# Taking the two joined steps fifth and sixth in the mixing stage, with their joining and parting cut into portions

## The chip, the cores and the metric

The kernel runs on one core of a Trainium2 chip. What is measured is the time of one execution on the device, in microseconds (us); the runs before the change have a median of 2587.52 us. The core has a matrix engine (PE, with its weight loads shown apart as PEld), a vector engine (DVE), a scalar engine (ACT), a general engine (POOL) and an engine that only issues transfers (SP). Each takes its own instructions in program order and waits on semaphores for the others.

## The reference

The input x is 4 images of 64 channels of 256 x 256, float32. Four layers follow each other. Layers 0, 2 and 3 are long separable convolutions with a filter that a small network makes, plus a per-channel multiple of the input. Layer 1 is a wavelet mixing layer, and the change lies there:

```
f1 = haar2d(x)                                  # Haar transform along both axes
acc = 0
for i in range(2):
    f3 = f1 * v[i]                              # per position
    f4 = einsum('bchw,oc->bohw', f3, conv_w[i]) # 64 x 64 over the channels
    acc += sign(f4) * relu(abs(f4) - tau[i])    # soft threshold
y = haar2d(acc, inverse=True) + x
```

## The kernel before

The four images are worked as two groups of two. Phase A does layer 0 and the forward transform, phase B the mixing of layer 1, phase C the inverse transform and layers 2 and 3. Phases A and C go by rounds of two channels, 32 rounds to a group; phase B goes by 64 steps of coefficient rows, all channels at once, so phase B of a group needs all rounds of phase A of that group, and phase C needs all of phase B. The coefficients go through DRAM in between (`coef`, `mixed`).

No scheduler orders the instructions. `beside(main, side, lead, tail)` writes the order out: it runs the main list of small pieces (a matmul block, an eviction, a few transform operations), and puts the pieces of the side list evenly in between. Phase B of group 0 is the side list of the second half of phase A (from here: **stage 0**, about 431 to 1050 us). Phase B of group 1 is the side list of phase C of group 0 (**stage 1**, about 1150 to 1900 us). In stage 0 404 side pieces lie among 270 main pieces (10 to a round); in stage 1 404 lie among 514 (18 to a round).

A step s has two units, u = 2s and 2s + 1, one for each of the two matrices. A unit u has three pieces, written u.0, u.1 and u.2:

- u.0: DVE `multiply(u)` (L626) takes the matmul result times v; DVE `less(u-1)` (L646) subtracts tau; POOL `add(u-2)` (L669 and L670 on the first unit of a step, L666 on the second) sums into the step's tile `gt`; SP stores a finished step (L675).
- u.1: PE `mix(u+1)` (L607), whose PSUM tile has one buffer, so that it waits for `multiply(u)`; ACT `sign(u)` (L632) into a tile of the ring `m` (3 buffers); DVE `threshold(u-1)` (L651); loads of v.
- u.2: ACT `magnitude(u)` (L641); on first units ACT `exchange(s)` (L657), a swap of partition halves into a tile of the ring `other` (2 buffers).

The ring `m` is freed by `add`: normally `sign(u)` takes the tile that `add(u-3)` let go. The ring `gt` has 3 buffers and is freed by the store.

Steps 0 and 1 hold coefficients for which the row transform is not finished. They are **joined** ahead of the mixing (16 DVE operations on 64 x 256, lines 579 to 586) and **parted** after it (8 POOL operations on 64 x 512, lines 592 to 599). The join is one side piece ahead of `mix(0)`. The part is in piece 6.0, in one go between `add(4)` and the next side piece, and borrows a tile of the ring `m`; the stores of steps 0 and 1 follow it.

In stage 1 the second unit of a step is left raw: the matmul result is copied to SBUF (L623), stored (L683), and thresholded in phase C. Only steps 0 and 1 have both units done in place (units 0 to 3); for them v of the second matrix is loaded into the ring `raw` at the start, and a tile of zeros (L681, a POOL memset) is stored in place of the raw result.

Main work around it: in stage 0 each round of phase A has a burst of 16 POOL operations (L344, L346), begun by the residual on DVE (L464), 1.9 us each for the first two, then shorter; DVE also evicts (L477). In stage 1 each round of phase C has 16 POOL operations of the inverse transform (L385) that grow from 0.2 to 2.5 us and end in the tile `ci`, which PE needs in the next round (L308, `c0ps`); DVE evicts the convolutions (L867).

Of the kernel before, what the change touches and what calls it, by code (L numbers as in the profile page):

```python
# [41 lines left out]
F32 = mybir.dt.float32  # L42
AF = mybir.ActivationFunctionType
ALU = mybir.AluOpType
# [3 lines left out]
P = 128  # L48
B, C, N = 4, 64, 256
# [16 lines left out]
GROUPS = 2  # L66
NB = B // GROUPS
# [3 lines left out]
PAD = 128  # L71
# [2 lines left out]
HALVES = 2 * ROUNDS  # L74
STEPS = C
FULL = 2

A_PIECES = 2 * BLOCKS + 2
C_PIECES = 4 * BLOCKS + 2
# [2 lines left out]
W = 2 * N  # L82
# [16 lines left out]
def conv_haar_kernel(  # L99
    ctx: ExitStack, tc: tile.TileContext, x, zT, w1, wbd, cols, wo, decay, wo_first, decay_first, bias, forward, inverse, wrow, pack, v, v_rows, out  # L100
):
    nc = tc.nc
# [186 lines left out]
    def half(r):  # L289
        return slice(r * ROW, (r + 1) * ROW)  # L290
# [113 lines left out]
    def run(ops, count):  # L404
        for _ in range(count):
            next(ops, None)
# [117 lines left out]
    def phase_b(grp):  # L524

        units = 2 * STEPS
        mixers = []

        def raw(u):
            return grp == GROUPS - 1 and u % 2 == 1 and FULL <= u // 2 < STEPS  # L530
        st = [dict() for _ in range(STEPS)]
        un = [dict() for _ in range(units)]
        pieces = []

        def step_of(ap, s, images):

            n = NB * W
            at = ap.offset + s // 2 * PAIR + s % 2 * P // CI * n
            rows = bass.AP(ap.tensor, at, [[n, P // CI], [STEPS // 2 * PAIR, CI], [1, n]])
            return rows, images.rearrange("p b w -> p (b w)")  # L540
# [9 lines left out]
        def load_v(s):  # L550
            if s >= STEPS:
                return
            d = st[s]
            d["v"], d["tau"] = [], []

            def fetch(first, count, tag):
                n = 2 * count * W
                t = bp.tile([P, count, 2, W], F32, tag=tag, name=f"{tag}_{grp}_{first}_{s}", bufs=3)
                at = v.offset + s * P * (4 * W + PAD) + first * 2 * W
                rows = bass.AP(v.tensor, at, [[4 * W + PAD, P], [1, n]])  # L560
                nc.sync.dma_start(t.rearrange("p i k w -> p (i k w)"), rows)
                d["v"] += [t[:, i, 0] for i in range(count)]
                d["tau"] += [t[:, i, 1] for i in range(count)]

            fetch(0, 2 if grp < GROUPS - 1 else 1, "v")
            if grp == GROUPS - 1 and not raw(2 * s + 1):
                fetch(1, 1, "raw")

        def four(name, at, b):

            tiles = [st[s][name] for s in range(2)]
            tiles.append(bp.tile([P, NB, W], F32, tag="m", name=f"spare_{name}_{grp}_{b}", bufs=3))
            return [t[at, b, bass.ts(h, N)] for t in tiles for h in range(2)]

        def join(image):

            a, b, c, d, t, u = four("f", half(image), image)
            op = nc.vector.tensor_tensor
            op(t, a, b, ALU.add)
            op(b, a, b, ALU.subtract)  # L580
            op(u, c, d, ALU.add)
            op(d, c, d, ALU.subtract)
            nc.vector.tensor_scalar(c, b, math.sqrt(2.0), None, ALU.mult)
            nc.vector.tensor_scalar(d, d, math.sqrt(2.0), None, ALU.mult)
            op(a, t, u, ALU.add)
            op(b, t, u, ALU.subtract)

        def part():

            a, b, c, d, t, u = four("g", half(0), slice(0, NB))  # L590
            op = nc.gpsimd.tensor_tensor
            op(t, a, b, ALU.add)
            op(b, a, b, ALU.subtract)
            nc.gpsimd.tensor_scalar(u, c, math.sqrt(2.0), None, ALU.mult)
            op(a, t, u, ALU.add)
            nc.gpsimd.tensor_scalar(d, d, math.sqrt(2.0), None, ALU.mult)
            op(c, b, d, ALU.add)
            op(d, b, d, ALU.subtract)
            op(b, t, u, ALU.subtract)

        def mix(u):
            s, i = divmod(u, 2)
            un[u]["f4"] = bps.tile([P, NB, W], F32, tag="f4", name=f"f4_{grp}_{u}", bufs=1)
            for b in range(NB):
                for r in range(2):
                    q = r ^ b
                    nc.tensor.matmul(  # L607
                        un[u]["f4"][half(q), b, :],
                        mixers[0][half(r), bass.ts(i, C)],
                        st[s]["f"][half(r), b],  # L610
                        start=True,
                        stop=True,
                        tile_position=(r * ROW, q * ROW),
                    )
# [28 lines left out]
        def less(u):  # L643
            if raw(u):
                return
            nc.vector.tensor_tensor(un[u]["a"], un[u]["a"], both(u, "tau"), ALU.subtract)  # L646
# [12 lines left out]
        def add(u):  # L659
            s, i = divmod(u, 2)  # L660
            if raw(u):
                un[u].clear()
                return
            m = un[u]["m"]
            if i:
                nc.gpsimd.tensor_tensor(st[s]["g"], st[s]["g"], m, ALU.add)  # L666
            else:
                g = st[s]["g"] = bp.tile([P, NB, W], F32, tag="gt", name=f"gt_{grp}_{s}", bufs=3)
                nc.gpsimd.tensor_tensor(g[:, 0], m[:, 0], st[s]["f"][:, 0], ALU.add)  # L669
                nc.gpsimd.tensor_tensor(g[:, 1], m[:, 1], st[s]["other"], ALU.add)  # L670
            un[u].clear()

        def store(s):
            to, g = step_of(mixed[grp], s, st[s]["g"])
            nc.sync.dma_start(to, g)  # L675
            st[s].clear()

        def store_raw(s):
            if s < FULL:
                t = st[s]["raw"] = bp.tile([P, NB, W], F32, tag="raw", name=f"none_{grp}_{s}", bufs=3)  # L680
                nc.gpsimd.memset(t, 0.0)  # L681
            to, g = step_of(unshrunk, s, st[s]["raw"])
            nc.sync.dma_start(to, g)  # L683

        def piece(u, j):

            s, i = divmod(u, 2)
            if j == 0:
                if u < units:
                    multiply(u)  # L690
                if 0 < u <= units:
                    less(u - 1)
                if 1 < u <= units + 1:
                    add(u - 2)
                if i == 0 and s == 3:
                    part()
                    store(0)
                    store(1)
                if i == 0 and s > 3 and not raw(2 * s - 3):
                    store(s - 2)  # L700
                if i and raw(2 * s - 1):
                    store(s - 1)
            elif j == 1:
                if u + 1 < units:
                    mix(u + 1)
                if u < units:
                    sign(u)
                if i and s < STEPS and grp == GROUPS - 1:
                    store_raw(s)
                if 0 < u <= units:  # L710
                    threshold(u - 1)
                if i == 0 and s > 0:

                    load_v(s + 2)
                    if grp < GROUPS - 1:
# [254 lines left out]
    bp = pool("b", 2, during)  # L970
# [4 lines left out]
    a, head = a[-2 * A_PIECES :], A_PIECES + BLOCKS  # L975
# [4 lines left out]
    bp = pool("b2", 2, during)  # L980
# [133 lines left out]
```

## Time and profile before

| | |
|---|---|
| runs | 2587.52, 2591.82, 2584.11 us; median 2587.52 us |
| profiled execution | 2585.35 us in all, span 2583.6 us from its first to its last instruction |
| mean granted TensorE clock | 0.977 |
| busy share of the span | PE 90%, DVE 71%, ACT 51%, POOL 80% |
| DMA, mean over the span | 265 GB/s |

The page gives busy time by engine, then the span in 40 slices of 64.6 us with the busy share of each engine in tenths. Below it is the chain that ended last, by engine: PE 60%, DVE 14%, POOL 10%, DMA 6%. Other views give the busy time of each engine in a stretch, the list of waits with their totals, and the instructions of one engine in order of time. In the timeline a line has start, duration, engine, source line, operation, tiles, and in brackets how long the engine sat idle before it and what released it. In the list of waits the numbers are the total in us, how often, and the longest.

### The profile page before, as it was taken

To read this page: it belongs to the slowest core of one execution; us is meant where nothing else is said; L and a number is where in the kernel's file an instruction comes from. 1 tells how busy PE (TensorE), PEld (TensorE's weight loads), DVE (VectorE), ACT (ScalarE), POOL (GpSimd) and SP (SyncE) were. 2 spreads that over 40 slices of the span, in tenths; PEclk is the share of its full clock that TensorE was granted. 3 is DMA by queue.
4 is the path that set the end of the run, shared out by engine and by line. 5 is a ranking of instruction groups with operands and counts; after the bars stand their busy time and mean duration, and the time that the engine had idled before them with its cause. 6 is when DMAs were issued, how large, how long until landed. Compare 5 with 4: busy or idle time off the path is not lost.

```text
span 2583.6 us, 118458 instructions
## 1 busy us (share of the span) xinstructions
PE 2319.3 (90%) x53292; PEld 1848.1 (72%) x53292; DVE 1823.0 (71%) x2049; ACT 1324.7 (51%) x2187; POOL 2064.4 (80%) x2428
## 2 busy tenths in 40 slices
PE   5999999678888888757999999999989999999999
PEld 4877877444444444546777778777789998999998
DVE  2555445799999999646677777766757777777763
ACT  1221212566666666325666666666655655655552
POOL 1898887899989999767676777766779999999991
PEclk8999999899999999978999999999999999999999
DMA  7676998699999999555988999988876666666653
GB/s 210 216 244 234 298 309 283 243 342 323 337 340 316 351 321 330 182 194 194 331 301 309 317 320 323 313 306 297 288 233 211 223 213 212 221 216 208 219 166 111
DMA packets 203676, 685.23 MB, mean 265 GB/s; under 512 B 29289, under 2 KB 30826, under 8 KB 190755
## 3 DMA queue, kind: packets, MB, share of 16 engines
q1 hardware_dynamic: 203171, 677.67, 77.1%
q8 instruction: 418, 6.85, 1.1%
q14 instruction: 87, 0.71, 0.1%
HBM read 427.93 MB, written 249.63 MB: 262 GB/s over the span
## 4 chain that ended last, share of the span: by engine, by line
PE 60%; DVE 14%; POOL 10%; DMA 6%; issue 5%; ACT 3%; SPq 2%; DVEq 0%; ACTq 0%; POOLq 0%
PE c2c L296 11%; PE c2r L296 10%; PE c1r L296 9%; PE c1c L296 9%; PE a1ps L296 6%; PE a2ps L296 6%; PE f L607 4%; PE c0ps L308 4%; POOL fw L344 3%; DVE m L651 3%; POOL f L346 3%; DVE x L626 3%; DVE a L646 2%; PE a3ps L308 2%; DVE x L464 2%
## 5 line engine op out<-in xcount | busy, mean ns | idle before, releaser
L385 POOL TENSOR_TENSOR i<-i,g 128x16 f32<-128x16 f32 x744 | 431.5, 601 | 27.7 <-ACT g L362 0.6
L296 PEld LDWEIGHTS a2ps<-toep,ay 64*64 64x64 f32 x8192 | 305.5, 137 | 163.9 <-DVE f L477 86.4
L296 PE MATMUL a2ps<-toep,ay 64*64 64x128 f32 (+3 forms) x8192 | 357.7, 306 | 47.9 <-DVE f L477 42.3
L607 PE MATMUL f<-ft,mix 64*64 64x512 f32 x2048 | 297.3, 617 | 111.6 <-DVE x L626 94.3
L296 PEld LDWEIGHTS a1ps<-toep,x 64*64 64x64 f32 x8192 | 288.4, 134 | 89.7 <-issue 45.4
L296 PE MATMUL a1ps<-toep,x 64*64 64x64 f32 (+3 forms) x8192 | 337.6, 300 | 16.6 <-DMA x<-in_x 11.4
L296 PEld LDWEIGHTS c2c<-toep,ch 64*64 64x64 f32 x8192 | 300.0, 135 | 58.9 <-issue 19.1
L296 PE MATMUL c1r<-toep,z 64*64 64x192 f32 (+3 forms) x8192 | 319.0, 300 | 22.6 <-issue 11.9
L296 PEld LDWEIGHTS c1c<-toep,ch 64*64 64x64 f32 x8192 | 296.2, 134 | 57.8 <-issue 18.5
L296 PEld LDWEIGHTS c1r<-toep,z 64*64 64x64 f32 x8192 | 292.4, 135 | 59.2 <-issue 28.0
L296 PE MATMUL c2c<-toep,ch 64*64 64x256 f32 (+3 forms) x8192 | 314.7, 299 | 8.4 <-ACT ch L848 6.8
L296 PE MATMUL c1c<-toep,ch 64*64 64x128 f32 (+3 forms) x8192 | 310.3, 298 | 9.0 <-ACT ch L848 5.5
L669 POOL TENSOR_TENSOR gt<-m,ft 128x512 f32<-128x512 f32 x128 | 163.5, 1277 | 193.7 <-DVE m L651 188.8
L385 POOL TENSOR_TENSOR ci<-i,g 128x1024 f32<-128x1024 f32 x124 | 313.9, 2552 | 4.5
L444 ACT COPY ay<-a1ps 128x512 f32<-128x512 f32 x256 | 137.4, 589 | 351.2 <-PE a1ps L296 350.6
L296 PEld LDWEIGHTS c2r<-toep,cy 64*64 64x64 f32 x8192 | 287.9, 134 | 32.9 <-issue 15.2
L632 ACT ACTIVATE m<-x 128x1024 f32<-128x1024 f32 x194 | 206.1, 1062 | 205.3 <-DVE x L626 98.5
L296 PE MATMUL c2r<-toep,cy 64*64 64x192 f32 (+3 forms) x8192 | 310.1, 297 | 1.3 <-issue 1.1
L848 ACT COPY ch<-c2r 128x512 f32<-128x512 f32 x256 | 137.3, 591 | 280.2 <-PE c2r L296 279.5
L477 DVE TENSOR_TENSOR f<-a3ps,wrow_sb 128x512 f32<-128x512 f32 x256 | 161.3, 683 | 130.2 <-PE a3ps L308 130.2
L626 DVE TENSOR_TENSOR x<-f,v 128x1024 f32<-128x1024 f32 x192 | 233.5, 1216 | 22.1 <-PE f L607 20.5
L344 POOL TENSOR_TENSOR fw<-x 128x1024 f32<-128x1024 f32 x64 | 122.2, 1910 | 150.4 <-DVE x L464 137.9
(83 smaller groups left out, 3976.8 us busy)
## 6 DMA issues: line engine op xcount, KB each, us to landing
toep<-filt SPq DMA_DIRECT2D x384, 224.0 KB, 5.3
ft<-coef SPq DMA_DIRECT2D x128, 512.0 KB, 7.6
v<-in_v SPq DMA_DIRECT2D x64, 1024.0 KB, 10.1
mixed<-gt SPq DMA_DIRECT2D x128, 512.0 KB, 7.2
g<-mixed SPq DMA_DIRECT2D x256, 256.0 KB, 5.1
x<-in_x SPq DMA_DIRECT2D x128, 256.0 KB, 4.4
coef<-f SPq DMA_DIRECT2D x128, 256.0 KB, 4.0
x<-in_x SPq DMA_DIRECT2D x32, 1024.0 KB, 8.0
```

The costliest lines, as they stand in the source:

```text
L296: nc.tensor.matmul(ps[r][half(c), j % 2, k * ROW :], data[half(r), c, k, bass.ts(j, ROW)], t(r, c)[:, : N - k * ROW], start=k == 0, stop=k ...
L308: nc.tensor.matmul(ps[r][half(c)].rearrange("p h k -> p (h k)"), matrix[half(r)], pairs(r, c).rearrange("p h k -> p (h k)"), start=True, s ...
L344: nc.gpsimd.tensor_tensor(diffs, even, odd, ALU.subtract)
L346: nc.gpsimd.tensor_tensor(sums, even, odd, ALU.add)
L385: engine.tensor_tensor(to, s, d, op)
L444: later(lambda y=y, ps=ps: nc.scalar.copy(y, ps))
L477: later(lambda f=f, ps=ps, w=w: nc.vector.tensor_tensor(f, ps, w, ALU.mult))
L607: nc.tensor.matmul(un[u]["f4"][half(q), b, :], mixers[0][half(r), bass.ts(i, C)], st[s]["f"][half(r), b], start=True, stop=True, tile_posi ...
L626: nc.vector.tensor_tensor(un[u]["x"], un[u]["f4"], both(u, "v"), ALU.mult)
L632: nc.scalar.activation(un[u]["m"], un[u]["x"], AF.Sign)
L669: nc.gpsimd.tensor_tensor(g[:, 0], m[:, 0], st[s]["f"][:, 0], ALU.add)
L848: later(lambda y=y, ps=ps: nc.scalar.copy(y, ps))
```

## The change

The order of the steps becomes 2, 3, 4, 5, 0, 1, 6, ... 63. The two joined steps are then at positions 4 and 5 (`held`), units 8 to 11. Every load and store addresses a step through `order`. `join` and `part` become generators. The join runs 4 operations at a time in pieces 6.0, 6.1, 6.2 and 7.0; the part runs 2 at a time in pieces 13.1, 13.2, 14.0 and 14.1, and both stores follow in 14.2. The join's spare tile comes from the ring `other` and is allocated once, with one image's room; the part's spare still comes from the ring `m`. In stage 1 units 1, 3, 5 and 7 are now raw and units 8 to 11 are done in full; v of the second matrix for the two steps is loaded in pieces 7.2 and 9.2 rather than at the start. The side list has 403 pieces.

```diff
+LATE = 4
@@ phase_b
+        order = [*range(FULL, FULL + LATE), *range(FULL), *range(FULL + LATE, STEPS)]
+        held = range(LATE, LATE + FULL)
         def raw(u):
-            return grp == GROUPS - 1 and u % 2 == 1 and FULL <= u // 2 < STEPS
+            return grp == GROUPS - 1 and u % 2 == 1 and 0 < u < units and u // 2 not in held
...
-            n = NB * W
+            n, s = NB * W, order[s]
...
-            if grp == GROUPS - 1 and not raw(2 * s + 1):
-                fetch(1, 1, "raw")
...
+        def four(name, at, b, spare):
+            rows = [(st[s][name], b) for s in held] + [(spare, slice(0, spare.shape[1]) if b == slice(0, NB) else 0)]
+            return [t[at, b, bass.ts(h, N)] for t, b in rows for h in range(2)]
+        def join():
+            spare = bp.tile([P, 1, W], F32, tag="other", name=f"spare_f_{grp}", bufs=2)
             op = nc.vector.tensor_tensor
-            op(t, a, b, ALU.add)
+            for image in range(NB):
+                a, b, c, d, t, u = four("f", half(image), image, spare)
+                yield op(t, a, b, ALU.add)
+                yield op(b, a, b, ALU.subtract)
+                yield op(u, c, d, ALU.add)
+                yield op(d, c, d, ALU.subtract)
+                yield nc.vector.tensor_scalar(c, b, math.sqrt(2.0), None, ALU.mult)
+                yield nc.vector.tensor_scalar(d, d, math.sqrt(2.0), None, ALU.mult)
+                yield op(a, t, u, ALU.add)
+                yield op(b, t, u, ALU.subtract)
...
         def part():
+            spare = bp.tile([P, NB, W], F32, tag="m", name=f"spare_g_{grp}", bufs=3)
+            a, b, c, d, t, u = four("g", half(0), slice(0, NB), spare)
             op = nc.gpsimd.tensor_tensor
-            op(t, a, b, ALU.add)
+            yield op(t, a, b, ALU.add)
...
         def piece(u, j):
-                if i == 0 and s == 3:
-                    part()
-                    store(0)
-                    store(1)
-                if i == 0 and s > 3 and not raw(2 * s - 3):
+                if i == 0 and s > 1 and s - 2 not in held and not raw(2 * s - 3):
                     store(s - 2)
...
+                if i and s + 1 in held and grp == GROUPS - 1:
+                    fetch(s + 1, 1, 1, "raw")
+            if u == 2 * LATE - 2 and j == 0:
+                joining.append(join())
+            if u // 2 == LATE - 1:
+                run(joining[0], 4)
+            at = 3 * (u - 2 * (LATE + FULL) - 1) + j - 1
+            if at == 0:
+                joining.append(part())
+            if 0 <= at < 4:
+                run(joining[1], 2)
+            if at == 4:
+                for k in held:
+                    store(k)
...
-        pieces += [start] + [lambda: None] * 10 + [lambda: [join(b) for b in range(NB)], lambda: mix(0)]
+        joining = []
+        pieces += [start] + [lambda: None] * 10 + [lambda: mix(0)]
```

More of the change, by code (lines that the diff above doesn't have):

```diff
@@ L552, in load_v @@
                 return
[L553 to L563, printed above, removed]
@@ L565, in load_v @@
-            fetch(0, 2 if grp < GROUPS - 1 else 1, "v")
-            if grp == GROUPS - 1 and not raw(2 * s + 1):
-                fetch(1, 1, "raw")
[L569 to L577, printed above, removed]
-            op = nc.vector.tensor_tensor
[L579 to L586, printed above, removed]
+            st[s]["v"], st[s]["tau"] = [], []
@@ new lines, in load_v, with fetch @@
+            fetch(s, 0, 2 if grp < GROUPS - 1 else 1, "v")
+        def fetch(s, first, count, tag):
+            d, n = st[s], 2 * count * W
+            t = bp.tile([P, count, 2, W], F32, tag=tag, name=f"{tag}_{grp}_{first}_{s}", bufs=3)
+            at = v.offset + order[s] * P * (4 * W + PAD) + first * 2 * W
+            rows = bass.AP(v.tensor, at, [[4 * W + PAD, P], [1, n]])
+            nc.sync.dma_start(t.rearrange("p i k w -> p (i k w)"), rows)
+            d["v"] += [t[:, i, 0] for i in range(count)]
+            d["tau"] += [t[:, i, 1] for i in range(count)]
@@ L588, in part @@
         def part():
-            a, b, c, d, t, u = four("g", half(0), slice(0, NB))
+            spare = bp.tile([P, NB, W], F32, tag="m", name=f"spare_g_{grp}", bufs=3)
+            a, b, c, d, t, u = four("g", half(0), slice(0, NB), spare)
             op = nc.gpsimd.tensor_tensor
-            op(t, a, b, ALU.add)
[L593 to L596, printed above, removed]
@@ L597, in part @@
-            op(c, b, d, ALU.add)
-            op(d, b, d, ALU.subtract)
-            op(b, t, u, ALU.subtract)
+            yield op(t, a, b, ALU.add)
+            yield op(b, a, b, ALU.subtract)
+            yield nc.gpsimd.tensor_scalar(u, c, math.sqrt(2.0), None, ALU.mult)
+            yield op(a, t, u, ALU.add)
+            yield nc.gpsimd.tensor_scalar(d, d, math.sqrt(2.0), None, ALU.mult)
+            yield op(c, b, d, ALU.add)
+            yield op(d, b, d, ALU.subtract)
+            yield op(b, t, u, ALU.subtract)
@@ L678, in store_raw @@
         def store_raw(s):
-            if s < FULL:
+            if s in held:
                 t = st[s]["raw"] = bp.tile([P, NB, W], F32, tag="raw", name=f"none_{grp}_{s}", bufs=3)
```

## The prediction

> **What bounds the kernel.** I read the busy times by stretch first, to see which engine fills which stage, then the waits of both stages, then the timelines round the join and the part. Columns of the stretches: PE, PEld, DVE, ACT, POOL busy, then PE clock, DMA share, GB/s.
>
> ```profile
> 431.00:470.00 39.00, 29.48 (x496) 19.64 (x492) 33.84 (x46) 18.78 (x24) 25.36 (x34) 0.91 0.84 310
> 470.00:520.00 50.00, 32.89 (x488) 19.80 (x484) 35.64 (x37) 24.47 (x31) 45.52 (x52) 0.86 0.65 243
> 700.00:800.00 100.00, 81.68 (x1326) 49.33 (x1324) 95.64 (x100) 64.59 (x81) 91.13 (x105) 0.98 0.95 337
> 1150.00:1220.00 70.00, 54.52 (x1120) 42.62 (x1120) 51.55 (x51) 43.13 (x75) 53.84 (x49) 0.89 0.63 211
> 1300.00:1400.00 100.00, 92.44 (x2163) 73.34 (x2155) 70.40 (x67) 63.01 (x111) 71.09 (x82) 1.00 0.89 307
> ```
>
> Stage 0 is bound by DVE (95.6 of 100 us) with POOL (91) and the DMA (0.95) close behind. Stage 1 is bound by PE (92); DVE and POOL have 30% free. The first two rows and the fourth show what the beginning of each stage loses.
>
> ```profile
> ACT m L632 <- POOL gt L670: 37.0, 25, 6.5
> DVE a L646 <- ACT a L641: 32.8, 38, 6.0
> ACT m L632 <- POOL gt L599: 6.5, 1, 6.5
> ```
>
> ```profile
> PE c0ps L308 <- POOL ci L385: 10.0, 1, 10.0
> PE f L607 <- DVE ft L586: 2.1, 2, 1.8
> ```
>
> In stage 0 the two 6.5 us waits of ACT for a tile of ring m (add(4) at 476.7, the part's last operation at 487.6) make DVE idle 5.74 and 5.96 us in the timeline. In stage 1 PE waits 10.0 us for ci, which stands behind the part on POOL:
>
> ```profile
> 1200.40 1.28 POOL L670 TENSOR_TENSOR gt<-m,other 128x512 f32<-128x512 f32 x1
> ...
> 1213.11 1.26 POOL L599 TENSOR_TENSOR gt<-_slice(0, 2, None)_16315 64x512 f32<-64x512 f32 x1
> 1214.34 3.51 POOL L385 TENSOR_TENSOR i<-i,g 128x512 f32<-128x512 f32 x2
> 1217.93 4.64 POOL L385 TENSOR_TENSOR ci<-i,g 128x1024 f32<-128x1024 f32 x2
> ```
>
> So both waits are real. The question is what replaces them. The join of stage 1 shows it, DVE first, POOL below:
>
> ```profile
> 1156.11 1.35 DVE L584 TENSOR_SCALAR ft<-ft 64x256 f32<-64x256 f32 x1
> 1157.38 1.49 DVE L585 TENSOR_TENSOR ft<-spare_f 64x256 f32<-64x256 f32 x1
> 1158.79 2.58 DVE L586 TENSOR_TENSOR ft<-spare_f 64x256 f32<-64x256 f32 x1
> 1161.40 0.42 DVE L579 TENSOR_TENSOR spare_f<-ft 64x256 f32<-64x256 f32 x1
> ```
>
> ```profile
> 1156.01 2.58 POOL L385 TENSOR_TENSOR i<-i,g 128x512 f32<-128x512 f32 x2
> 1158.66 2.42 POOL L385 TENSOR_TENSOR ci<-i,g 128x1024 f32<-128x1024 f32 x1
> ```
>
> Operations that take 0.29 to 0.42 us alone last until the POOL operation beside them ends; at 1161.4, with POOL idle, they are short again. The first image took 9.3 us, the second 2.9.
>
> [...]
>
> **Stage 0, part by part.** (a) Start. PE waited for the join until 438.31 and DVE multiplied at 440.31. Now mix(0) needs ft alone (landed about 432.2: issue 424.6, 7.4 to 7.7 us), but multiply(0) needs v, and the load issued at 427.9 took 13.0 us; the one ahead of it, 1 MB less at 419 GB/s, lands about 438.2. So 2.1 us at once; while DVE is short of work (3.2 us idle up to 467) PE's lead brings some 2 more. Take -4.0 (bounds -2, -6). (b) DVE's stalls go: 5.74 + 5.96, and 1.47 for a v load that stood behind the stores on SP (SP waited 20.1 us for L599): -13.2. (c) The join's 16 operations return in 6.0 to 7.0, where DVE is the bound: +5.9 (432.38 to 438.26). (d) [...] Piece 6.0 falls, by 403 side pieces on 270, on the main piece that begins the POOL burst. Behind the residual DVE does threshold, multiply, less (3.5 us); then POOL is at the end of its second 1.9 us operation, and 1.04, two of 1.27 (add(4)), 1.04, 0.61, 0.61, 0.4 ... and add(5) with 2.4 follow. Alternating one by one, the portions wait 0.3 + 1.04 + 1.27 + 1.27, then 0.5 + 0.6 + 0.4 + 0.4, then 0.3 + 2.4 + 0.3 + 0.25, then nothing (POOL waits for threshold(6)): +9.0 (bounds 0, +16: every operation behind one of 1.0 us). (e) The part, 10.9 us on POOL (476.66 to 487.56), in 13.1 to 14.1. Its place is kinder, behind the burst instead of in it, but sign(14) now takes the tile of add(12), which stands behind four part operations. POOL's sum from the burst's start: burst 4.85 + 2.26 + 1.1 + 0.78 + 0.45 + 0.42, add(9) to add(11) 7.3, four part operations 5.3, add(12) 2.55: 25.0 us. DVE comes to less(14), 13 side pieces of 1.65 us and one multiply later, at 22.7 and can go on at 25.0 + 2.1 (sign, magnitude): 4.4 us. sign(15) waits for the last part operation (30.3), about 1 us more, the next burst 0.6. Take +6.0 (bounds +2, +11). exchange(3) waits for add(4) (ring other) at 8.7 us, when ACT has nothing due: 0. Behind the held stores on SP (14.2) stand x, v and ft loads wanted a round or two units later; the wait, about 11 us, is shorter than the 20.1 before: 0. Step 7's gt tile waits for a store of 7 us under add(13) and a burst of 7.2: 0. Sum: -4.0 - 13.2 + 5.9 + 9.0 + 6.0 = **+3.7 us**.
>
> **Stage 1.** (f) PE's waits that go: 2.1 for the join, 10.0 for ci, about 2 for multiply at 1184 to 1211 (1.17, 0.61, 0.29), since units 1, 3, 5 are raw and POOL sheds two L666 (4.7) and the part (12.7): -14.1. (g) The join in 6.0 to 7.0 lies, by 403 on 514, on main pieces 11, 12, 14, 15 of a round, where POOL does its operations of 0.74, 1.5, 1.5, 2.4, 2.4. multiply(6) comes at 1192.2 (before: mix(6) on PE from 1194.6 to 1195.7, now 3.5 earlier by the terms of (f)). From 1193.4 the first portion waits 0.5 + 1.5 + 1.5 + 2.4 and works 1.6: 1200.9. The second waits once more, 2.4, and works 1.3: 1204.6. The third has POOL idle, 1.7: 1206.3. multiply(7), a raw copy, ends at 1207.5. mix(8) waits for it; PE has done three of its four c1c blocks by 1200.6 (before 1204.6): idle 6.9 us. mix(9) waits 2.3 more, behind the fourth portion, threshold(6) and two pairs of evictions: +9.2 (bounds 0, +16). (h) Units 8 to 11 in full: 4 x (1.23 + 1.62 + 1.59) = 17.7 us of DVE plus 5 of evictions in 22 us (four units of 5.5), where PE had no wait before: +1; v of the second matrix is issued 1.8 us behind the raw copy of unit 7, lands 5.8 to 7.6 us later, wanted after 11: +1 (0 to 3). Zero tiles, 2 x 0.95 on POOL, fit. (i) The part falls on pieces 3 to 7 of a round, where inverse operations are 0.3 us; POOL has 30% free for 12 pieces, ci is due 5 pieces later: 0 (up to 4). Sum: -14.1 + 9.2 + 2.0 = **-2.9 us**.
>
> Together +0.8 on the profiled 2585.35 us: 2586.1; that execution is 2.2 below the median of the runs shown, so I say **2587 us**.
>
> **Rivals.** *Faster*: DVE gets its short operations in between at nearly no cost, or POOL is not in long operations when they come. Without (d) stage 0 gives -5.3; without (g) stage 1 gives -12: 2585.4 - 17 = 2568 to 2570. For it: at 432 to 435, beside 0.25 us POOL operations, each join operation took 0.41 us. Against: the four lines above. *Slower*: [...] +7 and +7 over the forecast, 2601: one mechanism, in 6.0 to 7.0, deciding once a join operation loses over about 0.8 us on average (9.0 / 16 = 0.56 in the forecast for stage 0). For it: 2.58 us for one of 0.42. Against: POOL idles behind add(5). *Part at full price*: POOL's 9% of slack in stage 0 takes none of it up, (e) is 11: 2592. For it: two stalls of 11.7 us from 10.9 us of work before. Against: its place behind the burst.
>
> **Numbers.** Forecast (own range 2579 to 2596) 0.42, faster rival 0.30, slower 0.18, full price 0.10. A run of this kernel can't tell 0.3%, 7.8 us, from no change. The faster rival lies beyond it, the slower one too; of the forecast and the full price 0.10 runs over upwards. So faster 0.30, same 0.42, slower 0.28. The range, 2569 to 2602, leaves out about half of the faster rival's spread and a little above.
>
> **What would show it.** Join operations of 0.4 to 2.5 us at unit 6 in both stages, DVE without a gap there; PE waiting about 7 us for L623 before the eighth mix of stage 1; no 10 us wait for ci; one DVE gap of 4 to 5 us beside the part in stage 0 and none of PE in stage 1. Wrong if join operations keep to 0.42 us (then 2570), or if the multiplication of the first unit in stage 0 comes well before 438.

## The result, and the profile after

The changed kernel takes 2618.74 us (median of 4 runs, 2612.46 to 2621.67) against 2585.82 us before on the same chip (4 runs): a ratio of 1.0132, 95% interval 1.0108 to 1.0156. That is slower by about 33 us; forecast was 2587 us, no change, with a range that ended at 2602. The profiled execution took 2619.38 us (span 2616.3 us), 34.0 more than the one before.

The stretches of the kernel after, with the columns of those of before (stretch, length, then busy PE, PEld, DVE, ACT, POOL, then PE clock, DMA share, GB/s):

```profile
431.00:470.00 39.00, 24.12 (x456) 15.07 (x456) 34.28 (x34) 20.14 (x25) 28.00 (x29) 0.95 0.92 339
470.00:520.00 50.00, 32.79 (x500) 18.69 (x504) 45.10 (x52) 23.23 (x29) 36.08 (x43) 0.84 0.62 226
700.00:800.00 100.00, 72.74 (x1270) 49.42 (x1261) 88.35 (x91) 58.89 (x74) 82.35 (x89) 0.91 0.87 308
800.00:900.00 100.00, 80.80 (x1329) 47.95 (x1333) 95.82 (x100) 65.63 (x81) 91.11 (x102) 1.00 0.93 328
1150.00:1220.00 70.00, 52.54 (x1031) 42.41 (x1035) 27.29 (x31) 34.57 (x70) 38.58 (x62) 0.85 0.67 227
1250.00:1350.00 100.00, 81.19 (x1841) 62.26 (x1837) 67.97 (x58) 57.25 (x101) 86.03 (x79) 0.93 0.76 266
1300.00:1400.00 100.00, 92.46 (x2091) 71.25 (x2091) 65.81 (x62) 59.90 (x106) 70.71 (x83) 0.95 0.92 327
```

Between 470 and 520 us DVE now works 45 us where it worked 36: the stalls that the forecast wanted gone are gone. But between 700 and 800, far behind the last joined or parted tile, DVE is down from 95.6 to 88.4 us and POOL from 91 to 82, and from 800 on both are back. A stretch in which no joined or parted tile is worked has become slower. In stage 1 the stretch 1250:1350 has POOL at 86 and PE at 81 us, where the kernel before had 70 and 95:

```profile
1250.00:1350.00 100.00, 94.56 (x2202) 78.24 (x2202) 68.29 (x68) 63.75 (x112) 69.94 (x78) 1.00 0.88 305
```

The waits of PE in the kernel after from 1150 to 1400 us say why (total, times, longest):

```profile
PE c0ps L309 <- POOL ci L386: 10.6, 1, 10.6
PE f L609 <- DVE raw L625: 9.6, 4, 6.1
```

The wait for `ci` that was to go is there again, 79 us later in the span (1301.7 us against 1222.6).

Where the difference arises shows best along one sequence of instructions that both kernels have. Start of the same residual of phase A (four to a round) or of phase C (eight to a round), after less before, worked out from the two traces:

| place | difference |
|---|---|
| residual A 132 (420 us), ahead of all that differs | -3.9 us |
| multiply of unit 0 | -5.7 |
| residual A 148 / 152 (520 / 544 us; in between lies the part) | -4.5 / +4.6 |
| residual A 188 / 252 (756 / 1114 us) | +24.1 / +24.1 |
| residual C 0, about 1135 us | +23.8 |
| residual C 16 / 32 (1228 / 1280 us in the kernel before) | +15.3 / +28.0 |
| residual C 496 (2555 us in the kernel before) | +32.8 |

The first row says that this execution was 3.9 us ahead before it came to anything that differs. The executions of the other kernels below stand between 2.7 us ahead and 1.4 behind at that point. Such a lead is carried along: in the four of them whose stage 0 is that of the kernel before, it changes by 1.0 to 1.4 us until the end of stage 0. So what stage 0 costs is counted from residual A 132 here, and what stage 1 costs from residual C 0. Stage 0 costs 28.0 us (-3.9 to +24.1): the beginning, up to residual A 152, where all the moved work lies, 8.5, and the rounds behind it 19.5. Stage 1 costs 9.0.

**What slows the quiet rounds.** From 598 to 756 us six rounds of phase A take 26.1 to 26.3 us instead of 23.5 to 23.7. Four more take 24.8 to 25.0: the two ahead of them, the one behind them, and one at 491 us. The order of the operations on DVE within a round differs (rr two residuals, t threshold, x multiply, l less, ff two evictions, read off the timelines):

```
before                  rr t x l rr t x l t x l t ff x l ff t x l
after, 549 to 598 us    rr x l t rr x l t x l t x l ff t ff x l t
after, 598 to 756 us    rr x l t rr x l t x l t ff x l t ff x l t
after, from 780 us      rr t x l rr t x l t x l t ff x l ff t x l
```

The timelines of one such round of the kernel after, DVE first, then POOL, then ACT (start, duration, operation, and in brackets the idle time before it and what ended it):

```profile
623.46 1.23 DVE L653 SCALAR_TENSOR_TENSOR m<-a,m 128x1024 f32<-128x1024 f32 x1
624.60 1.40 DVE L465 SCALAR_TENSOR_TENSOR x<-x,bias_sb,a2ps 128x512 f32<-128x512 f32 x2
625.92 1.22 DVE L628 TENSOR_TENSOR x<-f,v 128x1024 f32<-128x1024 f32 x1
627.05 1.22 DVE L648 TENSOR_TENSOR a<-a,v 128x1024 f32<-128x1024 f32 x1
628.39 1.23 DVE L653 SCALAR_TENSOR_TENSOR m<-a,m 128x1024 f32<-128x1024 f32 x1
629.53 1.40 DVE L465 SCALAR_TENSOR_TENSOR x<-x,bias_sb,a2ps 128x512 f32<-128x512 f32 x2
...
643.58 1.23 DVE L648 TENSOR_TENSOR a<-a,v 128x1024 f32<-128x1024 f32 x1 [3.06 <-ACT a L643]
```

```profile
624.83 2.36 POOL L668 TENSOR_TENSOR gt<-gt,m 128x1024 f32<-128x1024 f32 x1 [0.63 <-DVE m L653]
631.00 1.89 POOL L345 TENSOR_TENSOR fw<-x 128x1024 f32<-128x1024 f32 x1 [3.82 <-DVE x L465]
```

```profile
640.60 1.06 ACT L634 ACTIVATE m<-x 128x1024 f32<-128x1024 f32 x1 [3.74 <-POOL gt L672]
```

A round of the kernel before, the burst on POOL and the only stretch in which DVE idles:

```profile
617.41 2.37 POOL L666 TENSOR_TENSOR gt<-gt,m 128x1024 f32<-128x1024 f32 x1 [0.61 <-DVE m L651]
620.98 1.89 POOL L344 TENSOR_TENSOR fw<-x 128x1024 f32<-128x1024 f32 x1 [1.20 <-DVE x L464]
...
632.60 1.23 DVE L646 TENSOR_TENSOR a<-a,v 128x1024 f32<-128x1024 f32 x1 [0.92 <-ACT a L641]
```

In the kernel after, POOL's last sum before its burst is let go by the threshold at 623.46, and the burst itself by the second pair of residuals, at 629.53. In between DVE has a pair, a multiply, a less, a threshold and the pair itself; in the good order that stretch is a multiply, a less and the pair. One pair (1.40) and one threshold (1.23) more are 2.6 us, and POOL idles 3.82 us ahead of the burst where it idled 1.20 before. The late burst pushes the sums behind it, the sign on ACT waits 3.74 us for one of them, the less on DVE 3.06 us for the magnitude that follows, where it waited 0.92 before: so the round closes 2.6 us late, and the next begins in the same order. In the order of the second row the same wait of DVE is 1.86 to 2.00 us, and the round 1.3 us longer. This chain of waits is read off the timelines; what the experiments test is the order. Six times 2.6 and four times 1.3 come to 20.8 of the 28.0 us.

The order is that of the list. `beside` places 403 side pieces on 270 where it placed 404. The content of a piece sits one place earlier at the front of the list, two thirds of a main piece, and drifts to no offset at its end; until about 755 us that is enough to bring three thresholds of a round ahead of a pair of residuals or evictions that they stood behind.

### The profile page after: what moved, and what is told of

It is laid out like the page before. It is cut to its first block, busy times and chain, and to the rows that moved or that the text cites. A ratio compares the mean times of both kernels' runs of the same rounds, so it can differ in the third digit from the quotient of the medians.

```text
span 2616.3 us, 118463 instructions
## 1 busy us (share of the span) xinstructions
PE 2303.0 (88%) x53292; PEld 1870.1 (71%) x53292; DVE 1831.1 (70%) x2049; ACT 1324.6 (51%) x2187; POOL 2060.6 (79%) x2428
## 4 chain that ended last, share of the span: by engine, by line
PE 60%; DVE 16%; POOL 10%; DMA 5%; issue 5%; ACT 2%; SPq 1%; DVEq 0%; ACTq 0%; POOLq 0%
PE c2r L297 10%; PE c2c L297 10%; PE c1r L297 10%; PE c1c L297 9%; PE a1ps L297 6%; PE a2ps L297 5%; PE f L609 4%; PE c0ps L309 4%; DVE x L628 3%; POOL fw L345 3%; POOL f L347 3%; DVE a L648 3%; DVE m L653 3%; PE a3ps L309 2%; DVE x L465 2%
## 5 line engine op out<-in xcount | busy, mean ns | idle before, releaser
L609 PE MATMUL f<-ft,mix 64*64 64x512 f32 x2048 | 311.7, 635 | 144.4 <-DVE x L628 129.0
L297 PE MATMUL a2ps<-toep,ay 64*64 64x128 f32 (+3 forms) x8192 | 341.2, 305 | 34.0 <-DVE f L478 29.0
L297 PEld LDWEIGHTS c1c<-toep,ch 64*64 64x64 f32 x8192 | 304.2, 134 | 54.0 <-issue 23.3
L297 PEld LDWEIGHTS a1ps<-toep,x 64*64 64x64 f32 x8192 | 278.8, 134 | 85.6 <-issue 44.4
L297 PE MATMUL a1ps<-toep,x 64*64 64x64 f32 (+3 forms) x8192 | 323.0, 300 | 14.2 <-DMA x<-in_x 11.0
L297 PEld LDWEIGHTS c1r<-toep,z 64*64 64x64 f32 x8192 | 299.1, 135 | 50.4 <-issue 24.0
L297 PE MATMUL c1c<-toep,ch 64*64 64x192 f32 (+3 forms) x8192 | 314.3, 298 | 9.0 <-ACT ch L861 6.1
L297 PE MATMUL c2c<-toep,ch 64*64 64x128 f32 (+3 forms) x8192 | 314.7, 298 | 8.1 <-ACT ch L861 7.1
L297 PE MATMUL c2r<-toep,cy 64*64 64x128 f32 (+3 forms) x8192 | 311.1, 297 | 4.2 <-issue 4.2
```

What stands on the lines that cost most here:

```text
L297: nc.tensor.matmul(ps[r][half(c), j % 2, k * ROW :], data[half(r), c, k, bass.ts(j, ROW)], t(r, c)[:, : N - k * ROW], start=k == 0, stop=k ...
L609: nc.tensor.matmul(un[u]["f4"][half(q), b, :], mixers[0][half(r), bass.ts(i, C)], st[s]["f"][half(r), b], start=True, stop=True, tile_posi ...
```

## The experiments

Times are medians, ratios are to the kernel before on the same chip, with the 95% interval.

**Is it the count of pieces?** Two edits, one to each kernel. The rival was a lag that the part leaves behind.

```diff
 the changed kernel, 404 side pieces
-        pieces += [start] + [lambda: None] * 10 + [lambda: mix(0)]
+        pieces += [start] + [lambda: None] * 11 + [lambda: mix(0)]
 the kernel before, 403 side pieces
-        pieces += [start] + [lambda: None] * 10 + [lambda: [join(b) for b in range(NB)], lambda: mix(0)]
+        pieces += [start] + [lambda: None] * 9 + [lambda: [join(b) for b in range(NB)], lambda: mix(0)]
```

> The changed kernel with one more empty side piece ahead of mix(0), in both stages, so that each side list has 404 pieces again and every unit stands beside the main pieces that it stood beside before; the join and the part move with it. Theory A (places): the slow rounds of stage 0 (about 26 us each for phase A rounds 38 to 47, instead of 23.6) come from where the 403 pieces fall among the main pieces, which gives DVE and ACT another order. Then all rounds of stage 0 but those with the join and the part take 23.6 us, stage 0 is within 8 us of before, and the ratio to the kernel before is 1.002 to 1.006. Theory B (lag): POOL, 10.9 us late by the part while it is 91% busy, stays late and keeps the rounds slow. Then they are slow here too and the ratio is 1.010 to 1.014.

> The kernel before with one empty side piece fewer in both stages, and nothing else changed: join and part as before, 403 pieces. Theory A (places): the same order of DVE and ACT as in the changed kernel, slow rounds until about round 47, stage 0 +20 to +30 us, ratio 1.007 to 1.012. Theory B (lag): the part is where it was, so nothing keeps the rounds slow: ratio 0.998 to 1.002.

An empty piece more: 2597.75 us, 1.0050 (1.0032 to 1.0069). An empty piece less in the kernel before, nothing else: 2609.11 us, 1.0108 (1.0075 to 1.0141). The stretches 700 to 800 us, the changed kernel with 404 first, the kernel before with 403 second:

```profile
700.00:800.00 100.00, 81.69 (x1326) 49.32 (x1324) 95.58 (x100) 64.58 (x81) 91.22 (x105) 0.98 0.95 337
```

```profile
700.00:800.00 100.00, 71.90 (x1233) 48.05 (x1227) 87.77 (x91) 58.92 (x74) 82.31 (x93) 0.91 0.87 303
```

The first is the row of the kernel before, nearly to the digit; the second that of the kernel after. With 404 POOL's wait ahead of the burst is back to that of the kernel before:

```profile
617.37 2.37 POOL L668 TENSOR_TENSOR gt<-gt,m 128x1024 f32<-128x1024 f32 x1 [0.61 <-DVE m L653]
620.93 1.90 POOL L345 TENSOR_TENSOR fw<-x 128x1024 f32<-128x1024 f32 x1 [1.19 <-DVE x L465]
```

This is shown, then. One empty piece less costs stage 0 of the kernel before 22.8 us (1.9 ahead at residual A 132, 20.9 behind at 252), in rounds of the same orders and lengths as in the kernel after; one more brings stage 0 of the changed kernel from 28.0 down to 2.7 (2.7 ahead to level). Of these 25.3 us the ten rounds above are 20.8, and 4.5 lie in the round with the join (residual A 140 to 144: 36.6 us with 403, 32.2 with 404). In stage 1 the count isn't the cause: the kernel before with 403 is 20.7 us behind at residual C 0 and at C 496. The lag of the part as a cause falls, since in the kernel before with 403 the part is where it was and the slow rounds come all the same.

**Each group alone.** The edit makes the lag of the held steps a value of the group, 4 in one and 0 in the other; a group with lag 0 keeps the join as a piece of its own ahead of `mix(0)`, and so 404 pieces, and the part in piece 6.0.

```diff
+        lag = LATE if grp in (0,) else 0        # and (1,) in the second kernel
-        order = [*range(FULL, FULL + LATE), *range(FULL), *range(FULL + LATE, STEPS)]
-        held = range(LATE, LATE + FULL)
+        order = [*range(FULL, FULL + lag), *range(FULL), *range(FULL + lag, STEPS)]
+        held = range(lag, lag + FULL)
...
```

> The change in group 0 alone; group 1 (stage 1) has the order, the join, the part and the 404 pieces of the kernel before. Both theories: stage 0 is 24 us longer, stage 1 as before: ratio 1.008 to 1.010. If stage 1 only inherits a loss from stage 0, the whole 1.013.

> The change in group 1 alone; group 0 (stage 0) is as before. Stage 1 loses about 8 us by the trace of the changed kernel (PE waits 6 us for the raw copy behind the join and 10.6 us for ci behind the part, and saves 10 us elsewhere): ratio 1.002 to 1.005. If the loss of stage 1 came from a late start in stage 0, 0.998 to 1.001.

Group 0 alone: 2615.78 us, 1.0128 (1.0103 to 1.0153), more than the 1.008 to 1.010 expected. Its stage 0 costs 28.4 us (0.2 ahead at residual A 132, 28.1 behind at 252), like that of the kernel after; the 24 us of the expectation were too few by the early lead. Stage 1 inherits no loss, though the ratio is the one forecast for that: the trace loses nothing behind residual C 0 (+28.4 there, +25.3 at C 496). Group 1 alone: 2594.54 us, 1.0043 (1.0013 to 1.0072), as expected. The two add up to 1.0171, more than the 1.0132 of both together, which the intervals allow. In stage 1 the second kernel leads by 12.1 us at residual C 16 (3.0 of it at C 0 already) and has lost it at 32 (+0.6); it ends 5.4 us behind. PE's waits from 1150 to 1600 us in it have the loss:

```profile
PE c0ps L309 <- POOL ci L386: 10.6, 1, 10.6
PE f L615 <- DVE x L634: 7.7, 9, 2.9
...
PE f L615 <- DVE raw L631: 5.9, 4, 4.5
```

**What stage 1 pays for.** Group 1 alone again, once without the part and once without the join of its two held steps.

```diff
 without the part
-            if 0 <= at < 4:
+            if 0 <= at < 4 and not grp:
 without the join
-            if u // 2 == LATE - 1:
+            if u // 2 == LATE - 1 and not grp:
```

> The change in group 1 alone, with the part of group 1's two held steps left out: their results are stored unparted, and the 8 POOL operations (10.5 us) of stage 1 are gone. Without that cut the same kernel stood at 1.0043 of before; in its profile it led by 12.1 us at residual C 16, and behind the PE wait of 10.6 us on the inverse (c0ps on ci) it was 0.6 us behind at residual C 32. Theory C (the part's POOL time is what stage 1 pays: it keeps the inverse, and so PE, waiting): the wait on ci of about 10 us is gone, residual C 32 leads by 8 to 12 us, and most of that lasts to the end: 0.996 to 1.000 of before. Theory D (the wait on ci belongs to the second round of phase C, as in the kernel before, which has one of 10.0 us without any part near it; the part lies in its shadow): the wait stays at 8 us or more and the ratio at 1.003 to 1.005.

> The change in group 1 alone, with the join of group 1's two held steps left out: the 16 DVE operations between the pieces of stage 1 are gone, the part is done. Theory C (the part is what stage 1 pays): the PE waits on the raw copies (5.9 us with the join) go, but the wait on ci of about 10 us stays; ratio 1.001 to 1.004 of before. Rival [...]: the wait on ci falls under 4 us and the ratio to 0.996 to 1.000.

Without the part: 2582.06 us, 0.9972 (0.9954 to 0.9989). The same list of waits holds none for `ci`; residual C 16 to 32 loses 3.5 us where it lost 12.7 with the part, and the lead at C 32 is 6.8 us (2.9 of it at C 0 already), a little less than theory C gave. At C 496 2.4 are left:

```profile
PE c1r L297 <- ACT z L861: 10.9, 1, 10.9
PE f L615 <- DVE x L634: 8.3, 9, 2.5
...
PE f L615 <- DVE raw L631: 6.6, 4, 4.6
```

Without the join: 2586.64 us, 0.9992 (0.9979 to 1.0005). The waits on the raw copies fall from 5.9 to 1.0 us, the one on `ci` stays at 10.6. The ratio lies a little under what theory C gave, so the join costs somewhat more than its waits on PE; but the wait on `ci` is the part's, so D falls, and the rival, by which the join holds the inverse back, too. D's ground was not so either: in the kernel before the part ends at 1214.4 us, just ahead of the inverse that PE waits for until 1222.6, so that the wait there stood behind a part as well.

**Can stage 0 keep its lead?** With 404 pieces stage 0 leads by 9.1 us at residual A 148 and by 0.1 at 152, with the part in between: it costs 9.0 (the 7.6 us at residual A 144, of which the expectations speak, are not yet the whole lead). Two kernels with 404 pieces: the part cut into 16 operations over eight pieces with a spare tile of its own, and the part of group 0 left out.

```diff
 part over eight pieces
-            spare = bp.tile([P, NB, W], F32, tag="m", name=f"spare_g_{grp}", bufs=3)
+            spare = bp.tile([P, 1, W], F32, tag="spare", name=f"spare_g_{grp}", bufs=1)
+            for image in range(NB):             # the eight operations for each image
...
-            if 0 <= at < 4:
+            if 0 <= at < 8:
...
-            if at == 4:
+            if at == 7:
 no part in group 0
-            if 0 <= at < 4:
+            if 0 <= at < 4 and grp:
```

> The changed kernel with 404 side pieces, and its part cut into 16 operations for one image each, two to a piece over eight pieces (13.1 to 15.2) instead of two whole ones to a piece over four, with a spare tile of its own that takes no slot of ring m; the stores go out in the last of the eight pieces. With the part in four pieces this kernel stood at 1.005: stage 0 led by 7.6 us at residual A 144 and by 0.1 at 152. Theory E (the part costs by its lumps: a burst of phase A that waits behind two long operations and a slot of ring m that is held): stage 0 keeps 4 us or more of the lead, ratio 1.001 to 1.003. Theory F (POOL is 91% busy in stage 0, so 10.5 us more on it fit nowhere within a few rounds): the lead at residual A 160 is 0 to 2 us, ratio 1.004 to 1.006.

> The changed kernel with 404 side pieces and with the part of group 0's two held steps left out: they are stored unparted, and stage 0 loses 8 POOL operations (10.5 us). With the part it stood at 1.005, and the lead of 7.6 us at residual A 144 was gone at 152. If the part alone takes the lead back (theories E and F alike), the lead of about 7.5 us stands from residual A 152 to the end of stage 0, and the ratio falls by 7.5/2585 to about 1.002. If the lead is lost to a standing order of the two instruction streams that any delay falls back to, it is gone here too, and the ratio stays at 1.005.

Over eight pieces: 2595.75 us, 1.0035 (1.0023 to 1.0046); residual A 152 is 3.1 us *behind*, so theory E falls and stage 0 pays 11.8 us for the part (8.7 ahead at residual A 148), more than F's forecast of a lead of 0 to 2 us. The ratio doesn't tell it from the kernel with four pieces, since the intervals overlap. Without the part: 2586.52 us, 0.9995 (0.9978 to 1.0011), below the 1.002 expected; the lead of 6.9 us stands from residual A 148 to the end of stage 0, so no standing order takes it. The profiled execution of that kernel took 2592.6 us, 6 more than its median: differences along a trace tell where time goes, the ratios how much. Small differences that gather slowly tell nothing: the kernel with 404 pieces and this one have the same stage 1, and from residual C 32 to C 496 the first loses 4.5 us and the second 7.3; group 0 alone, whose stage 1 is that of the kernel before, gains 4.1 there.

**Is there a place where the two are free?** If POOL's 30% of slack in stage 1 (busy 71 of 100 us between 1300 and 1400) could swallow the part anywhere but beside an early round, the middle of the stage should do; and the end of stage 0 should be free of the full engines.

```diff
+        lag = (0, 30)[grp]                      # and (62, 30) in the second kernel
...
-        pieces += [start] + [lambda: None] * 10 + [lambda: mix(0)]
+        pieces += [start] + [lambda: None] * (11 if lag else 10) + [lambda: run(join(), 16)] * (not lag) + [lambda: mix(0)]
...
 second kernel, part of group 0: four operations to a piece
+            at *= 1 + (lag > LATE and not grp)
-                run(joining[1], 2)
+                run(joining[1], 4 if not grp else 2)
```

> The change in group 1 alone, with the two held steps 31st and 32nd of group 1 instead of fifth and sixth, and 404 side pieces there; group 0 as before. At fifth and sixth this stood at 1.0043: it gained 9 to 12 us at the start of stage 1 and lost them to the part beside the second round of phase C (wait on ci 10.6 us). Theory C' (the part only costs there because it meets the inverse of a round whose PE work is due; in the middle of the stage POOL is 71 to 74% busy and swallows it): the lead of about 10 us at residual C 16 stands at residual C 32 and 48, the wait on ci is under 4 us, and at most 5 us are lost near 1500 us: 0.996 to 0.999 of before. Theory G (the lead isn't worth anything by itself: the second round of phase C and the rounds behind it end when their own inputs allow): residual C 48 is within 3 us of before, ratio 0.999 to 1.003.

> As the kernel with 31st and 32nd in group 1, and in group 0 the two held steps are last (63rd and 64th), with 404 side pieces; the part of group 0 then runs four operations to a piece behind the last sums of the stage. With the part left out of group 0, stage 0 kept a lead of 6.9 us. Theory F (in stage 0 DVE is 95% and POOL 91% busy, so join and part cost what they take wherever they are, except behind the stage's last pieces): stage 0 leads by 7 us at residual A 152 and keeps 3 to 7 us of it; then 0.994 to 0.998 of before. Rival (the end of stage 0 is as dear as its start, since phase A's last rounds and phase C's first loads wait there for the stores of the held steps): the lead at residual C 0 is within 2 us of the kernel with group 0 as before, and the ratio is no lower than that kernel's.

Middle of stage 1: 2593.10 us, 1.0036 (1.0020 to 1.0052); both theories fall. The lead is 17.8 us at residual C 16, 23.0 at 96 (1466 us), still 11.4 behind the join (1475 to 1491 us) and gone behind the part (1532 to 1547 us): +3.0 at 128. The wait on `ci` has moved with the part; none of 10 us is left at the second round (PE, 1150 to 1600 us):

```profile
PE c0ps L309 <- POOL ci L386: 13.0, 2, 12.3
```

End of stage 0 as well: 2601.91 us, 1.0067 (1.0039 to 1.0095). Here stage 0 leads by 14.6 us with neither join nor part done, evenly from residual A 152 to 232; since it was 1.4 behind at A 132, 16.0 are gained. The join near the end takes 13.8 and the part 10.9 more, so that stage 0 ends 10.0 us behind. The part then stands ahead of a burst of phase A, and PE waits for it, in 1050 to 1150 us:

```profile
PE a2ps L297 <- DVE f L478: 18.0, 3, 10.2
PE a3ps L309 <- POOL fw L347: 8.3, 1, 8.3
```

Theory F falls in its exception, the quiet end. Its rival is right on the ratio, and short on the size: the start of phase C is 10.9 us later than with group 0 as before, not within 2.

**Less work in place of another place.** If the two cost what they take of DVE and POOL, then taking operations off these engines should pay. The scalings by the root of two go to ACT, which is busy about 65% of stage 0 (64.6 of 100 us between 700 and 800), in the kernel before and in the changed one with 404 pieces.

```diff
-            nc.vector.tensor_scalar(c, b, math.sqrt(2.0), None, ALU.mult)
-            nc.vector.tensor_scalar(d, d, math.sqrt(2.0), None, ALU.mult)
+            nc.scalar.mul(c, b, math.sqrt(2.0))
+            nc.scalar.mul(d, d, math.sqrt(2.0))
...
-            nc.gpsimd.tensor_scalar(u, c, math.sqrt(2.0), None, ALU.mult)
+            nc.scalar.mul(u, c, math.sqrt(2.0))
...
-            nc.gpsimd.tensor_scalar(d, d, math.sqrt(2.0), None, ALU.mult)
+            nc.scalar.mul(d, d, math.sqrt(2.0))
```

> The kernel before, with the scalings by the root of two on ACT: four of the join's 16 operations per group leave DVE (0.29 us each) and two of the part's 8 leave POOL (1.49 us each); places unchanged. Theory H (join and part cost close to what they take of DVE and POOL wherever they stand): 3 us per part and up to 1 us per join less, so about 6 to 8 us for both groups: 0.997 to 0.9985 of before. Rival (the chain of the part gets a crossing between two engines at each scaling and ACT's signs wait behind it): 1.000 to 1.003.

> The changed kernel with 404 side pieces and the scalings of join and part on ACT. With the scalings on DVE and POOL it stood at 1.005. Theory H: the part takes back 3 us less of stage 0's lead (residual A 152 at about -3 us) and the wait on ci in stage 1 shrinks from 11.3 us to about 8: ratio 1.001 to 1.003. Rival (crossings and ACT's queue): 1.004 to 1.007.

The kernel before with it: 2578.99 us, 0.9984 (0.9970 to 0.9998), the lowest ratio of any kernel here that does the whole computation, and small. The changed one with 404: 2587.96 us, 1.0014 (0.9997 to 1.0032), from 1.0050. In its trace residual A 152 leads by 3.7 us (about 3 expected): the part costs 6.0 us from residual A 148 where it cost 9.0. The wait on `ci` is 7.9 us (about 8 expected). One part scaling takes 0.63 us on ACT where it took 1.49 on POOL. Both ratios lie where theory H put them, and the rival falls, in the kernel before by little.

## Why the prediction was wrong

**The step that failed** is the sum for stage 0, in what it left out. It priced the pieces that hold join and part, (a) to (e), and put every other round at nothing without a reason; it used 403 on 270 only to find where piece 6.0 falls. The same division moves all other pieces too. The missing term is 20.8 us in ten rounds without join or part, of 32.9 in all; with nothing changed but the count it is 22.8. The order on DVE in a round, and how long POOL idles ahead of each burst, could have been worked out from the kernel's list and the page before, since the two numbers 404 and 403 and the durations 1.40 and 1.23 were all there. In stage 1 it was step (i).

**Priced steps of stage 0.** Forecast +3.7. Measured, up to residual A 152: 8.5 in the kernel after, 2.6 with 404 pieces. That the sum is right to about 1 us where the order of the pieces is kept is luck: there (a) to (d) come out 4.1 us better than forecast and (e) 3.0 worse.

- (a) Start: -4.0 forecast, 2.1 of it at once. At once it was 1.8, the -5.7 less the 3.9 of before (1.7 to 2.2 in the six other kernels with the moved join). The v tile landed at 434.6, that is 438.5 without the early lead, where 438.2 was forecast. So the sign of being wrong that the forecast named, a multiplication well before 438, came true by the early lead alone.
- (b) The stalls of 5.74 and 5.96 us went, as said.
- (c) and (d) The join and its waits for POOL: 14.9 us forecast (5.9 + 9.0). The 16 operations took 13.7 us in all, and stretched as said; DVE of the kernel after:

```profile
462.98 1.92 DVE L580 TENSOR_TENSOR spare_f<-ft 64x256 f32<-64x256 f32 x1
...
471.17 0.41 DVE L586 TENSOR_TENSOR ft<-spare_f 64x256 f32<-64x256 f32 x1
...
473.03 2.56 DVE L582 TENSOR_TENSOR spare_f<-ft 64x256 f32<-64x256 f32 x1
475.63 0.42 DVE L583 TENSOR_TENSOR ft<-ft 64x256 f32<-64x256 f32 x1
```

  The same operation is 0.42 us where POOL is in short operations (0.47 us from 475.27, then 0.33) and 2.56 beside a sum of 2.54 on POOL (L668, from 472.77). The estimate of the forecast, that a join operation lasts about until the POOL operation beside it ends, was within 1.2 us in all. Other operations on DVE kept their length in stage 0: the threshold (L653), whose input `a` is in PSUM there, took 1.21 to 1.23 us each of 128 times, and in stage 1, where it reads `x` in SBUF, up to 3.37 us; no run here tells whether the place of the input is the cause. The faster rival, by which the join operations keep to about 0.42 us, is out.
- (a) to (d) together: -2.3 forecast. Measured at residual A 148: -0.5, with 1.3 of the slower order in it; -6.4 with 404 pieces.
- (e) Part: +6.0 forecast, 9.0 measured from residual A 148 to 152, in the kernel after and with 404 pieces alike. The idle stretch of DVE beside the part is 5.84 us (4.4 forecast); the one in the next burst is 3.22, where 0.6 was added.

**Stage 1.** Forecast -2.9, measured about +9.

- (f), (g): -4.9 forecast together; measured -8.5 from residual C 0 to 16. The wait of PE for the raw copy ahead of mix(8) was 6.1 us (6.9 forecast), all four 9.6 (9.2 forecast). That (g) came so near is partly luck. The join's 16 operations were stretched to 9.7 us from the 6.2 that they take at 432 to 438 us in the kernel before (the longest, 2.47 us at 1223.62, beside two on POOL that took 4.88 together from 1220.93), far less than the 8.3 us of waiting in the working; instead the third operation stood 3.75 us for a tile `ft` whose load is issued only one unit ahead, which was not foreseen.
- (h): +2.0 forecast; without the part, residual C 16 to 32 loses 3.5.
- (i) was put at 0, up to 4, and is the step that failed here: residual C 16 to 32 loses 12.7 us, 9.2 more than without the part, and PE waits 10.6 us for `ci`. The part fell where it was said to fall, among the short inverse operations (POOL of the kernel after):

```profile
1271.20 1.26 POOL L594 TENSOR_TENSOR spare_g<-gt 64x512 f32<-64x512 f32 x1
1272.54 1.27 POOL L595 TENSOR_TENSOR gt<-gt 64x512 f32<-64x512 f32 x1
1273.77 0.23 POOL L386 TENSOR_TENSOR i<-i,g 128x16 f32<-128x16 f32 x1
...
1286.17 2.13 POOL L601 TENSOR_TENSOR gt<-spare_g 64x512 f32<-64x512 f32 x1
...
1296.97 4.65 POOL L386 TENSOR_TENSOR ci<-i,g 128x1024 f32<-128x1024 f32 x2
```

  That was no cover. The rest of the round's inverse stands behind the part on the same queue, POOL has no gap from 1271 to 1302, and a slack of 30% taken over 100 us says nothing of the chain that one round has to finish. The runs at other places (12.3 us in the middle of the stage) say the same, and the run without the part has no such wait.

The slower rival, 2601 us, is nearer the measured 2618.7 than the forecast, by luck: its cause was waits of the join operations for POOL at their upper bounds in both stages, and in stage 0 they stayed near the middle (13.7 us where 14.9 was forecast). *Part at full price* was the better picture: the part costs 9.0 us in four pieces, 11.8 in eight and 10.9 at the end of stage 0. Where the gain of the removed stalls went in stage 0 can be said with numbers: without join and part its beginning is 16.0 us shorter than before, and doing the two as fifth and sixth, with 404 pieces, costs 18.6 of it again. One addition of the forecast has a slip: 2586.1 and 2.2 are 2588.3, not 2587.

What stays open: 4.8 us that the kernel after loses behind residual C 32, spread over 1300 us, which one execution can't tell from the scatter between traces; why (f) gained more than forecast; and whether another count of pieces than 404 makes rounds shorter than 23.6 us, which wasn't tried.

## What to carry to other kernels

Where a list is spread over another by its length, a piece more or less shifts all of it: work out the order on each engine in an undisturbed round before and after, and pad with an empty piece to keep it. Work on an engine that is on the path of each round cost about its own duration, or more, at every place that was tried (in stage 0 the part, 10.9 us of POOL before, cost 9.0 to 11.8, and the join, 5.9 us of DVE before, 13.8 near the end); moving it exchanged one stall for another, and only taking some of it off that engine paid, by a ratio of 0.9984. Two executions can differ before they come to the changed code, here by 3.9 us: take that off before a difference further on is put down to the change. Average slack is no cover where a chain due in this round stands behind the moved work in the same queue: here POOL was busy 71 of 100 us in the kernel before, and PE waited 10.6 us in the kernel after.

## What the runs showed that was not expected

A round of phase A has three steady periods with the same instructions, 23.6, 24.9 and 26.2 us, each with its own order on DVE, and one empty piece in the list decides which comes. The kernel after stays in the slowest for six rounds, until the drift of the list turns the order back. With the slow order goes a lower granted clock of TensorE, 0.91 between 700 and 800 us against 0.98, though PE had less to do (73 against 82 us busy); no run here tells whether it adds anything.
